# A state-space recurrence on one core: ScalarE instead of GpSimd copies each step's last states

## The chip, the cores and the metric

The kernel runs on one core of a Trainium2 chip. The metric is the device time of one execution in microseconds (us). Before the change the median of three runs is 3077.14 us (3073.25 to 3079.84).

The engines of a core are called PE (TensorE's matmuls; its weight loads are PEld), DVE (VectorE), ACT (ScalarE), POOL (GpSimd) and SP (SyncE, which here only issues DMAs). Each takes its instructions from a queue of its own and waits for the others through semaphores.

## What is computed

A block of two layers on 2 x 2048 tokens of width 256, all in float32: attention with 16 heads plus a mixture of 8 experts, then a state-space layer plus a ternary linear layer. Only the state-space layer is touched. Cut to what matters:

```python
x = silu(causal_conv(x) + conv_b)                 # 512 channels
dt = softplus(dt_low @ dt_proj_w.T + dt_proj_b)
def step(h, (dt_t, B_t, C_t, x_t)):               # h: 512 channels x 16 states
    h = exp(dt_t * A) * h + dt_t * B_t * x_t
    y = sum_over_states(h * C_t)
    return h, y
y = scan(step) + x * D
return (y * silu(z)) @ out_proj_w.T
```

The recurrence runs along time, from the first token of a sequence to its last.

## The kernel before

**Pieces.** A sequence is cut into 4 chunks of 512 tokens. A chunk of one of the two sequences is a piece here (the code calls it a unit and counts it by `at`), so there are 8 pieces, 0 to 7, the two sequences in turn. The last states of a chunk have to reach the next chunk of the same sequence, two pieces later. They are kept in `carry[b]`, a small tile per sequence.

**Steps.** A piece is worked off in 16 steps n = 0 to 15, 128 steps G = 0 to 127 in the whole kernel. A step holds 4 x 512 values on each of the 128 partitions (128x2048), four channel groups side by side. Step G is made of

- `decays` (L1729), four ACT activations 128x511 that write exp(dt A) into `decay[G % 2]`;
- `spread_b` (L1740), a PE matmul that spreads B over the partitions into the PSUM tile `bb`;
- `product` (L1753), a DVE multiplication that writes uh = dt x B into PSUM;
- L1841, a DVE addition on 128x4 elements, which puts the states carried in from the chunk before (`c0`) into uh;
- the scan (L1843), one DVE instruction over 128x2048, which writes the states hh (three buffers);
- the copy (L1854) of the last column of each group, 128x4 elements, from hh to `carry[b]`; and behind it on POOL
- the multiplication of hh in place by C (L1855, POOL, 128x2048);
- `summed` (L1770), PE matmuls that sum hh over the states into `y`, issued one step later.

Every fourth step ACT copies the finished `y` out of PSUM (`taken`, L1782).

**What fills the time between.** While the steps of a piece run, the pieces ahead are made ready and the one behind is finished. `mix` gathers expert outputs (L1302, indirect DMAs issued by POOL; L1311 scales them on ACT; L1316 adds them on POOL), adds the residual (L1379 POOL) and normalises (L1389, L1390 ACT; L1391 DVE; L1396, L1399 ACT). `ahead` projects (L1426 ACT takes the result), convolves by matmuls (L1446; L1455 ACT takes the result), applies Silu (L1461), computes the low-rank dt (L1466 PE, L1474 and L1475 ACT, L1535 PE, L1540 ACT), softplus (L1551 to L1563 on ACT, L1556 and L1561 on DVE) and dt and dt x (L1581, L1584 on POOL), spills both to DRAM (L1569) and reads them back spread over the partitions (`dd`, L1694). `first` makes `c0` for four steps from `dd` and `carry` (L1710 POOL, L1717 ACT, L1720 POOL). `behind` gates the finished piece (L1590 POOL, in two parts, which read the tile `xs` of that piece) and projects it out. In the first piece dt and dt x of its first channels are spread by matmuls instead (L1517, taken by ACT and DVE at L1520).

**The order is written by hand.** The scheduler is switched off for this part, so the order of the program text is the order of each engine's queue. Tables (`kinds0` for the first piece, `kinds` for the others) say at which step n and at which of four places q = 0 to 3 of that step a generator (`mix`, `ahead`, `behind`) advances by one stage. The loop of step G issues, in this order: `spread_b(G + 1)`, two `decays(G + 1)`, the stages of place 0, L1841 and the scan of G, two more `decays(G + 1)`, the stages of place 1, the copy L1854, the multiplication L1855, `summed(G - 1)`, the stages of place 2, `product(G + 1)`, the stages of place 3, `taken(G - 1)`. Results of matmuls are taken out of PSUM one stage late, from two buffers.

Of the kernel before, what the change touches and what calls it, by code (L numbers as in the profile page):

```python
# [25 lines left out]
CH = 512  # L26
# [75 lines left out]
def tile_model(ctx: ExitStack, tc: tile.TileContext, t, out):  # L102
# [55 lines left out]
    with ExitStack() as c0:  # L158
# [176 lines left out]
        experts(tc, t, col, row, ident, ones, xa, xa_d, rot, rw, x_d, y_d, routes)  # L335

    mix_and_state_space(
        tc, t, col, row, ident, ones, rot, routes, sab, rw, y_d, ab_d, xa_d, out_tiles
    )
# [808 lines left out]
def mix_and_state_space(tc, t, col, row, ident, ones, rot, routes, sab, rw, y_d, ab_d, xa_d, out_tiles):  # L1148
# [10 lines left out]
    nc = tc.nc  # L1159
# [7 lines left out]
    with ExitStack() as ctx:  # L1167
# [90 lines left out]
        carry, tail = [], []  # L1258
# [367 lines left out]
        def behind(at):  # L1626

            (c, b), m_ = units[at], of[at]
            if at > 0:
                gated(at - 1, slice(0, NB - 1))  # L1630
            yield
            if at > 0:
                gated(at - 1, slice(NB - 1, NB))
            yield
            out = leave(at - 1) if at > 0 else iter(())
            for _ in range(4):
                next(out, None)
                yield
            for _ in out:
                pass  # L1640
            zs = m_["zs"] = one.tile(full, F32, tag="zs", name=f"zs_{b}_{c}")
            for m in range(NB):
                issued(
                    project(NB + m, m_["xnT"], f"z_{b}_{c}_{m}"),
                    lambda ps, m=m: nc.scalar.copy(zs[:, m, :], ps),
                )
                yield
            settle()
            nc.scalar.activation(zs, zs, AF.Silu)
            yield  # L1650
# [39 lines left out]
        def spread(at, m):  # L1690

            dd = two.tile([P, 2, 4, CH], F32, tag="dd", name=f"dd_{at}_{m}")
            for r in range(4):
                nc.sync.dma_start(dd[C4 * r : C4 * (r + 1)], of[at]["dd_d"][m])  # L1694
            of[at]["dd", m] = dd

        def c_rows(at, g):

            cc = bcp.tile([P, 1, CH], F32, tag="cc", name=f"cc_{at}_{g}")
            for r in range(4):  # L1700
                nc.sync.dma_start(
                    cc[C4 * r : C4 * (r + 1), 0, :], of[at]["c_d"][4 * g + r].partition_broadcast(C4)
                )
            of[at]["cc", g] = cc

        def first(at, m):

            m_ = of[at]
            a0 = one.tile([P, 4, 4], F32, tag="a0", bufs=2, name=f"a0_{at}_{m}")
            nc.gpsimd.tensor_tensor(  # L1710
                a0,
                a_neg[:, :, 4 * m : 4 * m + 4].rearrange("p q g -> p g q"),
                m_["dd", m][:, 0, :, 0].unsqueeze(1).to_broadcast([P, 4, 4]),
                ALU.mult,
            )
            yield
            nc.scalar.activation(a0, a0, AF.Exp)  # L1717
            yield
            c0 = one.tile([P, 4, 4], F32, tag="c0", bufs=2, name=f"c0_{at}_{m}")
            nc.gpsimd.tensor_tensor(c0, a0, carry[units[at][1]][:, 4 * m : 4 * m + 4, :], ALU.mult)  # L1720
            m_["c0", m] = c0
            yield
# [3 lines left out]
        def decays(G, q):  # L1726
            if G < NG:
                at, n = divmod(G, NU)
                nc.scalar.activation(  # L1729
                    decay[G % 2][:, q, 1:],  # L1730
                    of[at]["dd", n // 4][:, 0, q, 1:],
                    AF.Exp,
                    scale=a_neg[:, q, n : n + 1],
                )

        def spread_b(G):
            if G < NG:
                at, n = divmod(G, NU)
                bb = of[at]["bb", n] = ps_u.tile([P, 1, CH], F32, tag="bb", name=f"bb_{at}_{n}")
                nc.tensor.matmul(  # L1740
                    bb[:, 0, :],
                    lhsT=selb[B0:XR, (n % 4) * P : (n % 4 + 1) * P],
                    rhs=of[at]["b"][B0:XR, :],
                    start=True,
                    stop=True,
                )

        def product(G):

            if G < NG:  # L1750
                at, n = divmod(G, NU)
                uh = of[at]["uh", n] = ps_u.tile(full, F32, tag="uh", name=f"uh_{at}_{n}")
                nc.vector.tensor_tensor(  # L1753
                    uh, of[at]["dd", n // 4][:, 1], of[at]["bb", n].to_broadcast(full), ALU.mult
                )

        def summed(G):

            if G < 0:
                return  # L1760
            at, n = divmod(G, NU)
            m, g = divmod(n, 4)
            hh = of[at]["hh", n]
            if g == 0:
                of[at]["y"] = ps_y.tile([P, CH], F32, tag="y", name=f"y_{at}_{m}")
                nc.tensor.matmul(
                    of[at]["y"], lhsT=dmat[:, m, :], rhs=of[at]["xs"][:, m, :], start=True, stop=False
                )
            for q in range(4):
                nc.tensor.matmul(  # L1770
                    of[at]["y"][C4 * q : C4 * (q + 1), :],
                    lhsT=sel,
                    rhs=hh[:, q, :],
                    start=False,
                    stop=(g == 3),
                    tile_position=(0, C4 * q),
                )

        def taken(G):
            if G >= 0 and G % 4 == 3:  # L1780
                at, n = divmod(G, NU)
                nc.scalar.copy(of[at]["xs"][:, n // 4, :], of[at]["y"])  # L1782
# [23 lines left out]
        def steps(at, n, q):  # L1806
            for kind in places.get((at == 0, n, q), ()):
                next(flows[kind], None)

        starts = nothing  # L1810
        for G in range(NG):
            at, n = divmod(G, NU)
            (c, b), m_ = units[at], of[at]
            m, g = divmod(n, 4)
            more = at + 1 < len(units)
            if n == 0:
                flows = [
                    aheads[at + 1] if more else nothing,
                    behind(at),
                    mixes[at + 2] if at + 2 < len(units) else nothing,  # L1820
                    mixes[at + 3] if at + 3 < len(units) else nothing,
                    aheads[at + 2] if at + 2 < len(units) else nothing,
                ]
                if at == 0:
                    flows += [mixes[2], aheads[0], mixes[1]]
            if g == 0 and m + 1 < NB and G:
                spread(at, m + 1)
            if more and n == 12:
                spread(at + 1, 0)
            if more and m == NB - 1:  # L1830
                c_rows(at + 1, g)
            if g == 2 and G > 2 or G == 3:
                starts = first(at, m + 1) if m + 1 < NB else first(at + 1, 0) if more else nothing
            spread_b(G + 1)
            for q in range(2):
                decays(G + 1, q)
            if g >= 2 and G != 2:
                next(starts, None)
            steps(at, n, 0)
            uh = m_["uh", n]  # L1840
            nc.vector.tensor_tensor(uh[:, :, 0], uh[:, :, 0], m_["c0", m][:, g, :], ALU.add)  # L1841
            hh = m_["hh", n] = wk.tile(full, F32, tag="hh", bufs=3, name=f"hh_{at}_{n}")
            nc.vector.tensor_tensor_scan(  # L1843
                hh.rearrange("p q c -> p (q c)"),
                decay[G % 2].rearrange("p q c -> p (q c)"),
                uh.rearrange("p q c -> p (q c)"),
                0.0,
                ALU.mult,
                ALU.add,
            )  # L1850
            for q in range(2, 4):
                decays(G + 1, q)
            steps(at, n, 1)
            nc.gpsimd.tensor_copy(carry[b][:, n, :], hh[:, :, CH - 1])  # L1854
            nc.gpsimd.tensor_tensor(hh, hh, m_["cc", g].to_broadcast(full), ALU.mult)  # L1855
            summed(G - 1)
            if g == 2 and G > 2 or G == 3:
                next(starts, None)
            steps(at, n, 2)
            product(G + 1)  # L1860
            steps(at, n, 3)
            if G == 3:
                next(starts, None)
            taken(G - 1)
            if n == NU - 1:
                for x in flows[:3]:
                    for _ in x:
                        pass
# [98 lines left out]
```

## Time and profile before

The profile is that of one execution.

| | |
|---|---|
| median of the runs | 3077.14 us |
| the profiled execution's own time | 3080.93 us |
| its span, first to last instruction | 3079.2 us |
| state-space part: first scan starts, last scan ends | 2014.2 us, 3052.5 us |
| DVE busy, whole span | 2043.7 us (66%) |
| ACT busy, whole span | 1592.4 us (52%) |
| POOL busy, whole span | 1187.6 us (39%) |
| the copies L1854, all 128 together | 45.6 us |
| mean granted TensorE clock | 0.897 of full speed |

How to read it. In a timeline, a line gives the start in us from the span's beginning, the duration, the engine, the line of the code, the operation, the tiles written and read, shapes and the number of instructions merged; a bracket at the end gives idle time of the engine before it and what ended that idle time. In the list of groups, "x128 | 579.9, 4531 | 10.3" says 128 instructions, 579.9 us busy, 4531 ns each, 10.3 us of idle time just before them. A wait for several semaphores is put down to the one that came last. "The waits of a line" lists how long its engine sat idle before its instructions, and until which instruction.

### The profile page before, as it was taken

How to read it: one execution, taken by the hardware profiler on the slowest of the kernel's cores; microseconds unless marked ns; L12 is line 12 of the kernel's file. 1: busy time of each engine (PE TensorE's matmuls, PEld its weight loads, DVE VectorE, ACT ScalarE, POOL GpSimd, SP SyncE). 2: the span in 40 equal slices, each digit the busy share in tenths (PEclk: the TensorE clock that was granted, in tenths of full speed). 3: DMA queues.
4: the chain of work that ended last, by engine and by line, in shares of the span. 5: the costliest groups of instructions: out<-in, count | busy, mean ns of one | idle time of the engine just before them, and what ended most of it. 6: DMA issues, size and time to landing. Idle time of an engine off the chain costs nothing. (4 is left out here: it accounts for less than half of the span.)

```text
span 3079.2 us, 39986 instructions
## 1 busy us (share of the span) xinstructions
PE 2634.9 (86%) x15021; PEld 1493.3 (48%) x15021; DVE 2043.7 (66%) x2558; ACT 1592.4 (52%) x2546; POOL 1187.6 (39%) x934
## 2 busy tenths in 40 slices
PE   6887888999999999799999999577778888788747
PEld 4543433445444444488888888333333343333303
DVE  6576766888788888324111011258999999999996
ACT  3424555666566666422222222456766676666643
POOL 4313223010111011111111111247887978878775
PEclk9978988999999999899999999677887888879758
DMA  8843214112232220434345553323544535445350
GB/s 290 214 133 80 57 51 86 29 29 42 50 48 29 29 29 1 151 134 144 133 150 194 183 193 109 77 54 85 120 111 104 131 78 133 110 102 117 82 116 14
DMA packets 120614, 309.58 MB, mean 101 GB/s; under 512 B 28464, under 2 KB 70832, under 8 KB 102880
## 3 DMA queue, kind: packets, MB, share of 16 engines
q1 hardware_dynamic: 100496, 206.57, 28.3%
q0 software_dynamic: 18576, 99.24, 9.6%
q8 instruction: 122, 2.00, 0.3%
q10 hardware_dynamic: 1344, 1.16, 0.1%
q14 instruction: 76, 0.62, 0.1%
HBM read 228.51 MB, written 78.38 MB: 100 GB/s over the span
## 5 line engine op out<-in xcount | busy, mean ns | idle before, releaser
L758 ACT ACTIVATE p<-s 128x1024 f32<-128x1024 f32 (+3 forms) x640 | 563.2, 900 | 382.4 <-PE s L750 361.5
L665 DVE TENSOR_REDUCE best<-m 128x2 f32<-128x1024 f32 (+3 forms) x640 | 669.6, 1062 | 111.6 <-PE m L652 101.0
L1855 POOL TENSOR_TENSOR hh<-hh,cc 128x2048 f32<-128x2048 f32 x128 | 579.9, 4531 | 10.3
L1843 DVE TENSOR_TENSOR_SCAN hh<-decay,uh 128x2048 f32<-128x2048 f32 x128 | 565.9, 4421 | 23.8 <-ACT decay L1729 10.1
L705 PE MATMUL pv<-p,v 128*17 128x256 f32 (+1 forms) x4608 | 383.8, 379 | 49.0 <-POOL p L763 46.1
L763 POOL TENSOR_SCALAR_AFFINE_SELECT p<-p 128x256 f32<-128x256 f32 x256 | 103.3, 408 | 785.6 <-ACT p L758 784.5
L1729 ACT ACTIVATE decay<-dd,a_neg 128x511 f32<-128x511 f32 x512 | 332.9, 712 | 53.4 <-DVE hh L1843 52.8
L1118 ACT ACTIVATE hT<-h,b1s 128x256 f32<-128x256 f32 x296 | 137.7, 473 | 384.3 <-PE h L1111 384.3
L1132 DVE TENSOR_TENSOR yt<-o,b 128x512 f32<-128x512 f32 x37 | 25.6, 692 | 436.9 <-PE o L1124 436.9
L1753 DVE TENSOR_TENSOR uh<-dd,bb 128x2048 f32<-128x2048 f32 x128 | 293.6, 2294 | 21.5 <-PE bb L1740 11.6
L750 PE MATMUL s<-q,k 64*128 64x512 f32 (+3 forms) x1280 | 288.2, 437 | 22.9 <-DVE best L665 17.6
L652 PE MATMUL m<-k,q 64*128 64x512 f32 (+3 forms) x1280 | 281.6, 426 | 17.6 <-DVE best L665 8.9
L1111 PE MATMUL h<-xT,w 128*128 128x256 f32 x1184 | 276.1, 387 | 19.7 <-ACT hT L1118 8.1
L1124 PE MATMUL o<-w,hT 128*128 128x256 f32 x1184 | 262.7, 380 | 0.0
L1074 POOL DMA_INDIRECT w<-in_w,wrow x74 | 71.1, 961 | 479.2 <-PE h L1111 255.5
L1111 PEld LDWEIGHTS h<-xT,w 128*128 128x128 f32 x1184 | 226.7, 193 | 54.8 <-ACT hT L1118 8.5
L750 PE MATMUL s<-tops,onesr 64*128 64x512 f32 (+3 forms) x1280 | 248.5, 371 | 0.0
L1124 PEld LDWEIGHTS o<-w,hT 128*128 128x128 f32 x1184 | 225.7, 191 | 30.9
L1770 PE MATMUL y<-hh,sel 128*32 128x512 f32 x1024 | 162.1, 710 | 78.8 <-POOL hh L1855 78.6
L705 PEld LDWEIGHTS pv<-p,v 128*17 128x17 f32 x4608 | 107.9, 97 | 232.4 <-issue 113.5
L750 PEld LDWEIGHTS s<-q,k 64*128 64x128 f32 x1280 | 127.0, 188 | 168.1 <-DVE best L665 56.6
L652 PEld LDWEIGHTS m<-k,q 64*128 64x128 f32 x1280 | 129.3, 192 | 131.7 <-ACT p L758 68.1
(341 smaller groups left out, 3477.2 us busy)
## 6 DMA issues: line engine op xcount, KB each, us to landing
dd<-dd_d SPq DMA_DIRECT2D x120, 512.0 KB, 7.1
q<-qk_d SPq DMA_DIRECT2D x128, 128.0 KB, 5.1
k<-qk_d SPq DMA_DIRECT2D x128, 128.0 KB, 7.5
x_d<-zero SPq DMA_DIRECT2D x6, 1664.0 KB
xg<-x_d SPq DMA_DIRECT2D x37, 256.0 KB, 6.6
y_d<-yt SPq DMA_DIRECT2D x37, 256.0 KB
qk_d<-qp SPq DMA_DIRECT2D x16, 512.0 KB, 7.3
qk_d<-kp SPq DMA_DIRECT2D x16, 512.0 KB, 4.0
```

The costliest lines, as they stand in the source:

```text
L652: nc.tensor.matmul(ps[:, h, 0:n], lhsT=qT[hs, qs], rhs=kT[hs, c * CH : c * CH + n], start=True, stop=True, tile_position=(HP * h, 0),)
L665: nc.vector.tensor_reduce(best[:, i, :, c], ps[:, :, 0:n], AX.X, ALU.max)
L705: nc.tensor.matmul(pv[r0 : r0 + HS + 1, lo - f * HC : HC], lhsT=v[:, b * TPB + kb, 2 * pr + h, :], rhs=pt[:, h, lo:hi], start=(kb == 0), s ...
L750: nc.tensor.matmul(ps[:, h, off:CH], lhsT=(kT[hs, kb * P : (kb + 1) * P], onesr[hs, :])[i], rhs=(qT[hs, j * CH + off : (j + 1) * CH], tp[h ...
L758: nc.scalar.activation(pt[:, :, off:CH], ps[:, :, off:CH], AF.Exp, scale=float(HS) ** -0.5)
L1111: nc.tensor.matmul(ph, lhsT=w1[:, k * DF + f * P : k * DF + (f + 1) * P], rhs=xT[:, k, :], start=(k == 0), stop=(k == 1),)
L1124: nc.tensor.matmul(po[:, h, :], lhsT=hT[:, f, h * P : (h + 1) * P], rhs=w2[:, f * D : (f + 1) * D], start=(f == 0), stop=(f == NF - 1),)
L1729: nc.scalar.activation(decay[G % 2][:, q, 1:], of[at]["dd", n // 4][:, 0, q, 1:], AF.Exp, scale=a_neg[:, q, n : n + 1],)
L1753: nc.vector.tensor_tensor(uh, of[at]["dd", n // 4][:, 1], of[at]["bb", n].to_broadcast(full), ALU.mult)
L1770: nc.tensor.matmul(of[at]["y"][C4 * q : C4 * (q + 1), :], lhsT=sel, rhs=hh[:, q, :], start=False, stop=(g == 3), tile_position=(0, C4 * q),)
L1843: nc.vector.tensor_tensor_scan(hh.rearrange("p q c -> p (q c)"), decay[G % 2].rearrange("p q c -> p (q c)"), uh.rearrange("p q c -> p (q c)"),
L1855: nc.gpsimd.tensor_tensor(hh, hh, m_["cc", g].to_broadcast(full), ALU.mult)
```

## The change

One instruction per step moves from POOL's queue to ACT's.

```diff
             for q in range(2, 4):
                 decays(G + 1, q)
             steps(at, n, 1)
-            nc.gpsimd.tensor_copy(carry[b][:, n, :], hh[:, :, CH - 1])
+            nc.scalar.copy(carry[b][:, n, :], hh[:, :, CH - 1])
             nc.gpsimd.tensor_tensor(hh, hh, m_["cc", g].to_broadcast(full), ALU.mult)
             summed(G - 1)
```

The place in the program stays. In ACT's queue the copy of step G stands behind the `decays(G + 1)` and the stages of places 0 and 1, and ahead of those of places 2 and 3. It waits for the scan of step G, which writes what it reads. The multiplication L1855 overwrites hh in place and therefore waits for the copy; on POOL that was given by the queue, now it is a semaphore between ACT and POOL. `first` reads `carry` on POOL (L1720), so there is now such a wait there too, in both directions. The orders of PE, DVE and SP are the same as before, and no table load is added on ACT.

## The prediction

> **What bounds the kernel now.** I read the page first, then the waits of the copy's line L1854, then windows over single pieces, then the timelines of ScalarE (ACT), GpSimd (POOL) and VectorE (DVE) across a border between pieces. Only the stretch after 2014 us of the 3079.2 us span is touched.
>
> From the page, with count, busy us, mean ns:
>
> ```profile
> L1855 POOL TENSOR_TENSOR hh<-hh,cc 128x2048 f32<-128x2048 f32 x128 | 579.9, 4531 | 10.3
> L1843 DVE TENSOR_TENSOR_SCAN hh<-decay,uh 128x2048 f32<-128x2048 f32 x128 | 565.9, 4421 | 23.8 <-ACT decay L1729 10.1
> ```
>
> One piece (16 steps) in the windows view: width, then busy us of PE, PEld, DVE, ACT, POOL.
>
> ```profile
> 2575.00:2703.00 128.00, 105.25 (x347) 45.48 (x345) 118.31 (x65) 86.80 (x135) 106.28 (x57) 0.85 0.46 110
> ```
>
> DVE is the bound: 118.3 of 128 us, and about 0.27 us of short gaps per step make it nearly full. ACT has 41 us of room, POOL 22. So an engine that only sheds work gains little; whoever makes DVE wait costs time. The copy itself, from the waits of its line (duration min/median/max in ns):
>
> ```profile
> L1854 POOL COPY carry<-hh x128: 177/188/2167, 2018.8 to 3052.6; 128x4 f32<-128x4 f32 x128
> ...
>   DVE hh L1843: 147.0, 64
> ```
>
> Half the copies find POOL already waiting for the scan; there removing a copy gains nothing unless its replacement ends earlier.
>
> **Part by part: what leaves POOL.** 128 copies. Most cost 0.19 us plus 0.08 before the multiply behind them: 0.27. Eleven took 1.6 to 2.17, ten of them 2.16 to 2.17, always while a VectorE scalar_tensor_tensor (L1556, L1561) ran: at step 8 of one piece the copy ran 2632.99 to 2635.15, that instruction 2632.84 to 2635.10. The Trainium skill (SBUF — State Buffer, section Who interferes with whom) explains it: a VectorE instruction with two SBUF inputs shuts out a GpSimd one that reads SBUF, and ScalarE waits for nobody. Taken for the copy alone it promises 10 x 1.97 = 20 us of POOL. But the same rule catches the multiply behind it, which reads two SBUF tiles and began only 0.08 us after the copy. I take 0.27 us there too.
>
> **What ACT gets.** 128 copies of 128x4. Nearest rows: L1717, 128x16, 0.22 us; L1396, 128x1, 0.28. I take 0.22: 28 us in all, hidden in ACT's idle 41 us per piece, except where ACT is late.
>
> **The new wait.** The multiply L1855 overwrites hh, so it must now wait for ACT's copy. If ACT is idle that changes nothing: before, the multiply began 0.33 us after the scan (0.06 + 0.19 + 0.08); after, about 0.06 + 0.22 + 0.06. But the copy stands on ACT behind all of decays(G+1) and the work of places 0 and 1 of its step. From the instruction order and the timeline I took, per step, the end of ACT's last instruction ahead of the copy minus the scan's end. It is positive in about half of the steps. At step 15 it is 4.1, 7.0, 5.7, 7.2, 5.6, 1.5, 2.8, 0 us over the eight pieces. Border of pieces 3 and 4:
>
> ```profile
> 2566.67 1.33 ACT L1729 ACTIVATE decay<-dd,a_neg 128x511 f32<-128x511 f32 x2
> 2567.91 1.69 ACT L1311 ACTIVATE ys<-ys,wts 128x256 f32<-128x256 f32 x4
> 2569.50 0.57 ACT L1426 COPY xr<-in 128x512 f32<-128x512 f32 x1
> 2569.97 2.56 ACT L1729 ACTIVATE decay<-dd,a_neg 128x511 f32<-128x511 f32 x4
> 2572.43 0.57 ACT L1426 COPY xr<-in 128x512 f32<-128x512 f32 x1
> 2578.37 0.59 ACT L1782 COPY xs<-y 128x512 f32<-128x512 f32 x1 [5.37 <-PE y L1770]
> 2578.85 2.56 ACT L1729 ACTIVATE decay<-dd,a_neg 128x511 f32<-128x511 f32 x4
> 2581.56 0.69 ACT L1455 ACTIVATE xs<-cv,cols 128x512 f32<-128x512 f32 x1
> ```
>
> ```profile
> 2564.91 4.52 POOL L1855 TENSOR_TENSOR hh<-hh,cc 128x2048 f32<-128x2048 f32 x1
> 2569.40 3.43 POOL L1590 TENSOR_TENSOR zs<-xs,zs 128x1536 f32<-128x1536 f32 x1
> ...
> 2573.45 4.51 POOL L1855 TENSOR_TENSOR hh<-hh,cc 128x2048 f32<-128x2048 f32 x1
> 2577.93 2.36 POOL L1316 TENSOR_TENSOR ys<-ys 128x1024 f32<-128x1024 f32 x1
> 2580.24 1.28 POOL L1590 TENSOR_TENSOR zs<-xs,zs 128x512 f32<-128x512 f32 x1
> ```
>
> See that L1455 starts when the second L1590 ends: it overwrites what that reads. The copy of step 15 lands behind the four L1311, at 2569.6, so its multiply starts at 2569.85 instead of 2564.91. All behind it on POOL is back to back: L1590 ends at 2577.8, the next multiply at 2582.6, L1316 at 2584.9, the second L1590 at 2586.2: 4.7 us late.
>
> Here a rule speaks against the change: the skill (Perfetto Trace Analysis, note under Tensor Engine Instruction) calls ACT, DVE and GPSIMD strict FIFO. The row agrees: the decays at 2578.85 needed only the scan that ended at 2572.46, yet stood behind L1782. Were the copy free to pass, it would go at 2562.45 and this border would cost nothing; by the rule it costs what follows.
>
> **Where the 4.7 us go** (steps 1 to 8, piece 4). L1455 ends at 2587.0, the copy behind it at 2587.2, decays and the second L1455 at 2590.6; the scan of step 3 (2589.48 before) waits: **+1.2**. TensorE's second-next convolution waits for the first L1455 to free its PSUM tile, so convolution, y and the transpose slip 4.1 us; with them Silu, its two table loads and the decays of step 5, which end at 2606.65; the scan (2603.80) now could start at 2605.0: +1.65, **2.9** so far. The gate, xp (5.4 us) and dt matmuls are 4.3 to 4.5 late; their products wait for bb behind them in TensorE's queue, and uh of step 8 and the pn evacuation, which already waited 0.53 and 1.36 us for TensorE, move fully: **+3.7** by step 8. In pieces 2 and 5 the scan of step 5 waited for ACT already (0.65 us), so no slack softens it: **+4.4**. In piece 1 the slip at L1590 is 3.3 and 2.6 reach step 8. In pieces 6 and 7 the slip is at most 2.8 and covered.
>
> **A second wait.** At step 10 ACT loads the Sqrt table and computes L1389/L1390 just before the scan ends (L1390 2653.96, scan's end 2654.06). The copy is put ahead and holds them until after the scan: 0.28 + 0.22 + 1.28 + 0.30 + 0.2, so DVE's reciprocal L1391, first behind that scan, waits 2.2 us. Pieces 1 to 4 take this from later stalls: there POOL is 5 to 9 us behind at steps 11 to 13, and DVE waits 4.0 us for it at steps 14 to 16 anyway (1.41 + 1.21 + 1.42 in piece 4). Piece 5 has no such stall: +2.2. Piece 0 has it at step 12: +0.8.
>
> **The gain.** In pieces 1 to 4 the next piece's start hangs on POOL: multiply, xc, multiply, L1581, multiply, L1584, whose spill and reload feed L1710. Two copies lie in it: -0.55 each.
>
> **The first piece.** ACT reaches the copy of step 1 at 2038.6, 4.8 after the scan; the multiply ends at 2043.4, not 2040.1, and L1575, for which TensorE stood idle 8.6 us, is 3.3 late. Step 2's copy is late by 3.6 more behind the L1520, so L1581, L1584, the spill and L1422 are 6.8 late, and c0 (L1720), for which DVE waits 12.5 us at 2077.55, comes 6.7 late: **+6.7**. Step 13's late multiply delays L1710 and the Silu behind it: +0.6. With L1391: 8.1.
>
> **Sum.** Piece 0: 8.1; 1: 2.6 - 0.55 = 2.05; 2: 4.4 - 0.55 = 3.85; 3 and 4: 3.15 each; 5: 4.4 + 2.2 = 6.6; 6 and 7: 0. Together 26.9 us. The profiled execution took 3080.93 (span 3079.2 and 1.7 around it): 3107.8. The median of the runs shown is 3.8 lower, so 3104.
>
> **Rivals.** *Faster.* Place: POOL's chain at steps 8 to 14. If the late multiply of step 15 is absorbed, pieces 1 to 4 gain three to four copies each, 0.8 to 1.1 us: 3 to 5 us, 3073. For it: the page's chain of waits lists POOL carry with 1%. It decides where step 15's multiply slips less than about 1.2 us, the slack ahead of step 5's scan; the trace says 5.0. And the first piece's 6.7 us has no slack anywhere. Chance 4%.
> *Absorbed.* From steps 2 to 7 POOL waits 2.2 to 2.4 us per scan, three hh buffers leave a multiply some room, and the convolutions may catch up. Then only the first piece and L1391 in piece 5 are left, less the gain: 8.1 + 2.2 - 2.2 = 8, 3085; with less of the first piece, within 0.2%. Chance 14%.
> *Cascade.* ACT lateness breeds more: copies of steps 4 to 7 come 1 to 4 us after the scan now and later after the slip, y on TensorE waits, and the slip reaches step 8 at 7 us instead of 4: 4 x 3.5 more, and 3 in piece 1: 17 more, 3121. If a late multiply of step 7 then also holds off L1556, some 10 more. Chance 17%.
> *As summed*: 65%.
>
> **How the numbers follow.** About 0.2% (6 us) is what a measurement of this kernel can tell from no change. Faster 0.04; same 0.08 (part of the absorbed case); slower 0.88. The range, 3084 to 3128, takes in absorbed and cascade and leaves out the faster case and the tails. The copy's price, 0.19 to 0.28, moves the sum by under 3 us.
>
> **What would show it.** Right: POOL's L1855 preceded by idle time ended by ACT L1854; at step 15 that multiply 5 us later after its scan; in piece 0 DVE's waits before L1385 and before L1841 of step 4 grow by 3.3 us each, to 9 and 16; about 2 us before L1391 in pieces 1 to 5; more DVE time waiting for decays; last two pieces unchanged. The multiply of step 8 still starts 2.1 us or more after the scan. Wrong: the multiply of step 15 starts within 2 us of its scan, or piece length from 2316 to 2703 (129 us each) does not grow.

## The result, and the profile after

The changed kernel takes 3094.47 us (median of four runs, 3092.49 to 3099.28); the kernel before, run beside it, 3075.19. The ratio is 1.0063, with a 95% interval of 1.0047 to 1.0079: 19.4 us longer, 14.5 to 24.3. The profiled execution took 3099.28 us, its span 3097.6.

Groups of the page, after. The columns are count, busy us, mean ns, then idle time before and what ended it.

```profile
L1855 POOL TENSOR_TENSOR hh<-hh,cc 128x2048 f32<-128x2048 f32 x128 | 597.7, 4671 | 233.6 <-ACT carry L1854 193.0
L1843 DVE TENSOR_TENSOR_SCAN hh<-decay,uh 128x2048 f32<-128x2048 f32 x128 | 565.9, 4421 | 34.0 <-ACT decay L1729 20.3
L1753 DVE TENSOR_TENSOR uh<-dd,bb 128x2048 f32<-128x2048 f32 x128 | 293.6, 2294 | 13.8 <-PE bb L1740 3.0
```

POOL now stands idle 233.6 us ahead of its multiplication, 193.0 of them until the copy on ACT ends. Part of that was there before, as waiting for the scan ahead of the copy (147.0 us). What counts is DVE, the bound: it works as long as before (2044.0 us in the whole span, before 2043.7), so the loss is what its idle time grew by. Ahead of the scan that is 10.2 us (23.8 to 34.0), and what ACT's decays end of it doubled. Ahead of the reciprocal L1391 it is 10.0 more, 14.7 instead of 4.7, but ahead of L1753 it is 7.7 less (before: 21.5): a good part of the reciprocal's wait is given back later.

The waits of the copy's line, after; the first kept line is what ACT waits for ahead of it, the second who waits for it:

```profile
L1854 ACT COPY carry<-hh x128: 178/196/204, 2025.2 to 3069.6; 128x4 f32<-128x4 f32 x128
...
  DVE hh L1843: 156.9, 55
...
  POOL hh L1855: 193.0, 55
```

In 55 of 128 steps ACT is early and waits for the scan. In 55 steps POOL waits for ACT. No copy takes 2 us any more.

One piece in the windows view, piece 4 as before (width, then PE, PEld, DVE, ACT, POOL):

```profile
2587.00:2718.00 131.00, 103.39 (x343) 45.32 (x342) 118.78 (x66) 88.04 (x152) 103.44 (x41) 0.86 0.45 109
```

DVE's work is the same 118 us (118.78, before 118.31), but the piece is 3 us wider. The border of pieces 3 and 4 on ACT and on POOL, after:

```profile
2577.94 1.69 ACT L1311 ACTIVATE ys<-ys,wts 128x256 f32<-128x256 f32 x4
2579.54 0.18 ACT L1854 COPY carry<-hh 128x4 f32<-128x4 f32 x1
2579.62 0.58 ACT L1426 COPY xr<-in 128x512 f32<-128x512 f32 x1
...
2595.92 0.69 ACT L1455 ACTIVATE xs<-cv,cols 128x512 f32<-128x512 f32 x1 [7.35 <-POOL zs L1590]
2596.50 0.19 ACT L1854 COPY carry<-hh 128x4 f32<-128x4 f32 x1
2596.59 1.33 ACT L1729 ACTIVATE decay<-dd,a_neg 128x511 f32<-128x511 f32 x2
```

```profile
2579.80 4.54 POOL L1855 TENSOR_TENSOR hh<-hh,cc 128x2048 f32<-128x2048 f32 x1 [5.32 <-ACT carry L1854]
2584.28 3.48 POOL L1590 TENSOR_TENSOR zs<-xs,zs 128x1536 f32<-128x1536 f32 x1
2587.67 0.22 POOL L1430 COPY tail<-xr 128x12 f32<-128x12 f32 x1
2587.82 4.54 POOL L1855 TENSOR_TENSOR hh<-hh,cc 128x2048 f32<-128x2048 f32 x1
2592.29 2.37 POOL L1316 TENSOR_TENSOR ys<-ys 128x1024 f32<-128x1024 f32 x1
2594.60 1.28 POOL L1590 TENSOR_TENSOR zs<-xs,zs 128x512 f32<-128x512 f32 x1
```

This is the predicted chain. The copy of step 15 runs behind the four L1311. Its multiplication starts 5.7 us after its scan (before: about 2.5), POOL is back to back up to the second L1590, and when that ends L1455 goes on ACT, for which ACT has stood idle 7.35 us. Counted from the end of step 0's scan, the two L1590 end 4.9 and 4.3 us later than before, and L1455 starts 4.3 later; the prediction had 4.7. Counted from its own scan the multiplication of step 15 is only 3.2 us later, not 5: the copy came 5.5 us after that scan, not 7.2, while step 0's scan now follows that of step 15 more closely (8.4 us after it instead of 10.0).

**Piece by piece.** Lengths from the end of step 0's scan to that of the next piece's step 0, in us. To keep the chance of one execution apart from the change, both kernels were traced twice more (runs before_b, before_c, after_b, after_c below), so each figure is a mean of three traces.

| piece | before | after | difference | predicted |
|---|---|---|---|---|
| 0 | 166.40 | 171.10 | 4.7 | 8.1 |
| 1 | 127.90 | 130.66 | 2.8 | 2.05 |
| 2 | 128.93 | 130.09 | 1.2 | 3.85 |
| 3 | 127.75 | 130.65 | 2.9 | 3.15 |
| 4 | 128.49 | 130.89 | 2.4 | 3.15 |
| 5 | 124.00 | 129.33 | 5.3 | 6.6 |
| 6 | 119.24 | 119.15 | -0.1 | 0 |
| 7 (to its last scan) | 107.32 | 107.34 | 0 | 0 |

Together 19.2 us; the timed runs show 19.4. By halves: in pieces 1 to 5 the first eight steps grow by 3.1, 2.0, 4.0, 3.0 and 3.1; the last eight shrink by 0.3, 0.8, 1.1 and 0.6 in pieces 1 to 4 and grow by 2.2 in piece 5.

### The profile page after: what moved, and what is told of

The parts are those of the page before. It is cut to its first block, busy times and chain, and to the rows that moved or that the text cites. A ratio compares the mean times of both kernels' runs of the same rounds, so it can differ in the third digit from the quotient of the medians.

```text
span 3097.6 us, 40026 instructions
## 1 busy us (share of the span) xinstructions
PE 2636.1 (85%) x15021; PEld 1495.6 (48%) x15021; DVE 2044.0 (66%) x2558; ACT 1604.6 (52%) x2674; POOL 1161.6 (38%) x806
## 5 line engine op out<-in xcount | busy, mean ns | idle before, releaser
L1855 POOL TENSOR_TENSOR hh<-hh,cc 128x2048 f32<-128x2048 f32 x128 | 597.7, 4671 | 233.6 <-ACT carry L1854 193.0
L1753 DVE TENSOR_TENSOR uh<-dd,bb 128x2048 f32<-128x2048 f32 x128 | 293.6, 2294 | 13.8 <-PE bb L1740 3.0
```

The source lines that it names most:

```text
L1753: nc.vector.tensor_tensor(uh, of[at]["dd", n // 4][:, 1], of[at]["bb", n].to_broadcast(full), ALU.mult)
```

## The experiments

Three theories stood. **A**, the prediction's: the multiplication L1855 has to wait for copies that come late, above all that of step 15, and a copy put ahead of L1389 holds up the reciprocal. **B**: ACT's 28 us of added work are the price, wherever they lie. **C**: what stands behind the copy in ACT's queue is held while the copy waits for its scan. Us in this section are the ratio times the 3076 us of the kernel before, with the 95% interval.

**Step 15 alone (only15), and all but step 15 (not15).**

```diff
-            nc.gpsimd.tensor_copy(carry[b][:, n, :], hh[:, :, CH - 1])
+            if n == 15:            # not15: if n != 15
+                nc.scalar.copy(carry[b][:, n, :], hh[:, :, CH - 1])
+            else:
+                nc.gpsimd.tensor_copy(carry[b][:, n, :], hh[:, :, CH - 1])
```

> Only the copies of step 15 (8 of 128) go to ScalarE, the others stay on GpSimd. Theory A (a late copy holds up GpSimd's multiplication, and the late multiplication of step 15 holds up the convolutions of the next piece): the slip of steps 1 to 8 in pieces 1 to 5 stays, 13 to 14 us in the trace after the change, so about 3089, with the rises at steps 3 to 8 and none at step 11. Rival B (the copies' own time on ScalarE, 128 x 0.19 = 25 us): 8 copies, 1.5 us, 3077. Rival C (ScalarE's own later work is held behind the wait for the scan): nothing is held at step 15, where the copy itself comes late: 3075.

> All copies but those of step 15 go to ScalarE. Theory A: the first piece (4.3 us in the trace after the change) and the reciprocal at step 10 in piece 5 (2.2) stay, less 0.5 to 1 us of GpSimd's gain in each of pieces 1 to 4: about 3079, and pieces 1 to 4 no longer than before. Rival B: 120 of 128 copies, 23 us, 3097. Rival C: unchanged from all copies on ScalarE, about 3094.

Measured: only15 3090.48 us, ratio 1.0048 (1.0034 to 1.0062), +14.8 us (10.5 to 19.1). not15 3082.49 us, ratio 1.0015 (1.0005 to 1.0024), +4.6 (1.5 to 7.4). Eight copies make 14.8 us and the other 120 make 4.6, which together is the 19.4 of the whole change. The waits of only15's eight ACT copies:

```profile
L1855 ACT COPY carry<-hh x8: 181/183/197, 2179.4 to 3061.2; 128x4 f32<-128x4 f32 x8
...
  POOL hh L1858: 31.4, 8
```

Eight copies of 0.18 us make POOL wait 31.4 us. B is out: a sixteenth of the load brings three quarters of the loss. In not15 pieces 2, 3 and 4 are shorter than before (126.64, 126.97 and 126.54 us). Not all of that is POOL's gain: 0.7, 0.9 and 0.4 us of it lie in the last eight steps, where the prediction has that gain, and in pieces 2 and 4 another 1.6 in the first eight, in piece 2 from step 5 on, where TensorE ran faster (see the part on steps 1 to 8 below). Its piece 0, with no copy of step 15 on ACT, took 174.30 us, longer than in any of the three traces of the changed kernel.

**All but step 10 (not10)**, as above with `n != 10`.

> All copies but those of step 10 go to ScalarE. Theory A: the wait of 2.1 us before the reciprocal goes in pieces 1 to 5, but only piece 5 keeps the gain, since pieces 1 to 4 lose it to later stalls on GpSimd: 2.2 us less than with all copies on ScalarE, about 3092. Rival C: 2.1 us in each of five pieces, 10 less, about 3084. Rival B: 1.5 less, 3093.

Measured: 3096.71 us, ratio 1.0068 (1.0054 to 1.0082), +20.9 (16.6 to 25.2); a miss for A's number. In the trace the jump at step 11 is gone as A said (piece 5 is 127.05 us, not 129.3). But the last eight steps of pieces 1 to 4 shrink less: 68.3, 67.9, 68.4 and 67.8 us, where the changed kernel has 67.9, 67.5, 67.7 and 67.4. Together that is 1.9 us, against the 2.2 gained in piece 5. Step 10's copy is back in POOL's queue there; that this is what takes it back is argued, not tested. Nothing is left that can be measured.

**Wait and load apart (apart).** All copies are on ACT, as in the change. GpSimd multiplies 511 of the 512 columns; ACT scales the last column in place, behind its own copy. So the multiplication waits for nobody on ACT, while ACT has 128 instructions more than in the change.

```diff
-            nc.gpsimd.tensor_copy(carry[b][:, n, :], hh[:, :, CH - 1])
-            nc.gpsimd.tensor_tensor(hh, hh, m_["cc", g].to_broadcast(full), ALU.mult)
+            nc.scalar.copy(carry[b][:, n, :], hh[:, :, CH - 1])
+            nc.scalar.activation(hh[:, :, CH - 1], hh[:, :, CH - 1], AF.Copy, scale=m_["cc", g][:, 0, CH - 1 : CH])
+            ct = m_["cc", g][:, :, 0 : CH - 1].to_broadcast([P, NB, CH - 1])
+            nc.gpsimd.tensor_tensor(hh[:, :, 0 : CH - 1], hh[:, :, 0 : CH - 1], ct, ALU.mult)
```

> All copies go to ScalarE, but GpSimd's multiplication leaves out the last column (511 of 512 columns), and a second small ScalarE activation, behind the copy, multiplies that column by its C in place: so GpSimd no longer waits for ScalarE, while ScalarE waits and works as before and does one instruction more per step. The output is the same. Theory A: the slip at steps 1 to 8 and the first piece's loss go, the 2.2 us at the reciprocal in piece 5 and 0.8 in piece 0 stay, GpSimd's gain of 0.5 to 1 us per piece stays: 3072 to 3078. Rival B: twice the instructions, 25 to 50 us more than before: 3100 to 3125. Rival C: as with all copies on ScalarE, 3094.

Measured: 3074.16 us, ratio 0.9996 (0.9988 to 1.0004). The whole 19 us are gone. The multiplication's line in apart, with what its idle time waits for:

```profile
L1857 POOL TENSOR_TENSOR hh<-hh,cc x128: 4492/4532/6436, 2020.8 to 3054.8; 128x2044 f32<-128x2044 f32 x128
...
  DVE hh L1843: 148.9, 60
```

It waits for the scan, not for ACT. A stands; B and C fall as the main cause. C's part remains in small: from step 10 to 11 the scans still slip by 2.5 us, which is the reciprocal's wait; most of it is given back later in pieces 1 to 4, and in the time nothing is left over.

**ACT's load alone (load).** The kernel before, with 128 ACT copies of 128x4 from a constant tile, waiting for nothing (`idle` is a small tile set to 0 beforehand, which the cut leaves out).

```diff
+            nc.scalar.copy(idle[:, 1, :], idle[:, 0, :])
             nc.gpsimd.tensor_copy(carry[b][:, n, :], hh[:, :, CH - 1])
```

> The kernel before, whose copies stay on GpSimd, with 128 further ScalarE copies of 128x4 from a constant tile at the same place in the order: they wait for nothing and nobody waits for them. A (ScalarE's time doesn't matter, only what waits for the copy): 0.09 to 0.2 us each where ScalarE's decays are just in time, so 0 to 2 us, 3075 to 3077. B (ScalarE's load is the price): 3090 to 3095, as in the changed kernel.

Measured: 3076.88 us, ratio 1.0003 (0.9994 to 1.0011), at most 3.4 us by the interval. As A has it; B is out.

**The wait without the relief (both).** The kernel before, and beside each copy an ACT copy of the same elements to a tile that nobody reads. POOL's multiplication waits for it, and POOL sheds nothing.

```diff
             nc.gpsimd.tensor_copy(carry[b][:, n, :], hh[:, :, CH - 1])
+            nc.scalar.copy(idle[:, 1, :], hh[:, :, CH - 1])
```

> The kernel before, whose copies stay on GpSimd, and beside each a ScalarE copy of the same 128x4 out of hh into a tile that nobody reads: GpSimd's multiply waits for it as in the changed kernel, but GpSimd sheds nothing. A (the wait of the multiply makes the loss, and shedding a copy from GpSimd gives 0.5 to 1 us in each of pieces 1 to 4): the changed kernel's 3094.5 plus 2 to 4: 3096 to 3099. D (shedding the copies gains nothing): 3094 to 3095. B (shedding costs, for instance because carry is written by another engine): under 3090.

Measured: 3104.71 us, ratio 1.0097 (1.0082 to 1.0112), +29.8 (25.2 to 34.5): 10 us above the change, where A expected 2 to 4. The sign is A's, the size is not. In the trace the last eight steps of pieces 1 to 4 take 68.3, 68.4, 69.0 and 68.1 us, 3.3 more than in the changed kernel: the expected part. Another 4.5 lie in piece 0, 175.6 us to 171.1, but there one trace is a weak witness: ahead of L1556 in step 1 DVE waits 6.38 us, as in the first trace of before and in not15, and 4.57 in the three of the changed kernel. That is 1.8 of the 4.5. So shedding the copies is worth something in the first piece too (about 2 us, worked out below), and the timed runs say that it is worth more than I thought; where all 10 us come from is not settled.

**All but the first piece (notfirst)**, as only15 with `at > 0`.

> The 16 copies of the first piece stay on GpSimd, the other 112 go to ScalarE. A (each loss sits where one late copy lands, and the sums of the pieces are separate): the first piece's +4.8 us goes, pieces 1 to 5 lengthen as in the changed kernel (1.3, 1.4, 2.8, 2.5, 4.6), so about 3075 + 12.6 = 3088 to 3090, and DVE's waits before L1385 and before L1841 of step 4 stay at 5.8 and 12.5 us. B (ScalarE is simply loaded with 28 us): 112 of 128 copies, so 7/8 of 19.3 us: 3092. C (the loss grows with each late copy by way of the next piece): a punctual first piece also saves part of the later ones, under 3085.

Measured: 3086.57 us, ratio 1.0038 (1.0024 to 1.0052), +11.7 (7.4 to 16.0). The first piece's copies make some 8 of the 19 us. My expectation of 3088 to 3090 put the piece borders wrongly: step 15 of piece 0 belongs to these copies and its loss falls into piece 1. In the trace both happen: piece 0 is 165.85 us as before, and piece 1, which the change lengthens by 2.8, takes 126.86.

**Both ACT instructions later in the step (later).** As apart, with the two ACT instructions behind place 2 of the step.

```diff
             steps(at, n, 2)
+            nc.scalar.copy(carry[b][:, n, :], hh[:, :, CH - 1])
+            nc.scalar.activation(hh[:, :, CH - 1], hh[:, :, CH - 1], AF.Copy, scale=m_["cc", g][:, 0, CH - 1 : CH])
```

> All copies on ScalarE, GpSimd multiplies the first 511 columns of hh only, and a second ScalarE instruction scales the last column in place; both stand behind the third place of each step in ScalarE's order, not behind its second. Output as before. A (the multiply no longer waits for ScalarE, and behind place 3 the two instructions no longer stand between the Sqrt load and L1389/L1390): no jump of 2.1 us at step 11, the gain of 0.5 to 1 us in pieces 1 to 4 kept: 3070 to 3073, below both kernels. C (ScalarE's own order of place costs nothing or moves the stall elsewhere: sums of step n+3 or the buffer of hh wait for the last column): 3076 to 3085.

Measured: 3075.11 us, ratio 0.9995 (0.9987 to 1.0003). The jump at step 11 is gone, as A said (from step 10 to 11 the scans shift by -0.1 us against before, not +2.1), but the time misses A's 3070 to 3073: it is better than the change and cannot be told from the kernel before. Nor from apart: with the reciprocal's wait or without it, the time is the same, as not10 has it too. The gain in the last eight steps is under 0.4 us in pieces 1 to 3 and none in piece 4, not 0.5 to 1 each; why it is smaller than in the changed kernel, no run here shows.

**Each kernel traced twice more (before_b, before_c, after_b, after_c)**, unedited.

> The kernel before, unedited, for a second trace of it. A (the half-speed stretches of TensorE fall differently in each execution, so part of the shortfall of the predicted sum is the one trace it was read from): its scans stand 1.5 us or more earlier than in the first trace by the end of the first piece, and pieces 1 to 5 differ from the first trace by up to 2.6 us each, as in the kernel with 128 idle copies. E (the stretches belong to the kernel): every piece within 0.3 us of the first trace.

> The kernel before once more. As for the one ahead of it: A: first piece 0 to 1.6 us shorter than in the first trace, pieces 1 to 5 scattered by up to 2.6 us. E: within 0.3 us.

> The changed kernel, unedited, for a second trace of it. A: the first piece lengthens by 3 to 8 us against the first trace of before (four traces with its copies moved gave 4.8, 6.9, 3.4, 8.2), pieces 1 to 5 by 11 to 15 together, pieces 6 and 7 by nothing; the stretch from step 5 to step 8, which the prediction had at +0.8, scatters between -1 and +1.3. E: every piece within 0.3 us of its first trace.

> The changed kernel once more. As for the one ahead of it: A: first piece 3 to 8 us longer than in the first trace of before, pieces 1 to 5 together 11 to 15. E: within 0.3 us of its first trace.

Measured, one execution each: 3078.20, 3071.52, 3092.54, 3097.17 us. Neither theory holds for every piece. Pieces 2, 3, 4, 6 and 7 of before agree within 0.2 us over the three traces, so there E is right. Pieces 0, 1 and 5 of the first trace are 1.5, 2.8 and 1.5 us longer than the mean of the other two: the trace that I predicted from was a slow draw in three places. The changed kernel's pieces 1 to 5 make 11.0 and 11.4 us more than in the first trace of before, at the lower edge of what A gave.

## Why the prediction was right or wrong, point by point

**The cause was right.** The time is lost because POOL's multiplication waits for a copy that stands behind other work on ACT (apart takes that wait away and adds to ACT's work, and the loss goes), most of it at step 15 (only15), none of it through ACT's load (load). The rivals fall: Faster, because step 15's multiplication slips by 3 to 5 us; Cascade, because no slip bred more than 4.0 us by step 8 on the mean of three traces. Absorbed is true in part: pieces 2 and 5 pass on less than was said, as the next points show.

**The sum was 26.9 us and the traces give 19.2.** Of the 7.7 too many, 3.4 are in the first piece, 3.6 in steps 1 to 8 of the later pieces, 0.7 in the gain. The terms that were mis-sized:

*The first piece, 8.1 by the prediction, 4.7 by the traces.* DVE's waits in the first piece, before and then after:

```profile
2045.00 0.43 DVE L1385 BATCH_NORM_STATS2 st<-xc 128x6 f32<-128x256 f32 x1 [5.78 <-POOL xc L1379]
...
2077.55 0.17 DVE L1841 TENSOR_TENSOR uh<-uh,c 128x4 f32<-128x4 f32 x1 [12.53 <-POOL c L1720]
```

```profile
2046.05 0.43 DVE L1385 BATCH_NORM_STATS2 st<-xc 128x6 f32<-128x256 f32 x1 [8.90 <-POOL xc L1379]
...
2063.99 2.30 DVE L1753 TENSOR_TENSOR uh<-dd,bb 128x2048 f32<-128x2048 f32 x1 [1.54 <-PE bb L1740]
2081.82 0.17 DVE L1841 TENSOR_TENSOR uh<-uh,c 128x4 f32<-128x4 f32 x1 [15.54 <-POOL c L1720]
```

The two signs came nearly as written, 8.9 and 15.5 where 9 and 16 were said. That they were right and the sum was not has three reasons. First, the gain on POOL's side was counted in pieces 1 to 4 alone. With the wait and no relief (both) the first piece takes 8.2 us more than in the first trace of before, which has the same long wait in step 1: 3.2 at step 2, 3.4 at step 4, 1.4 at its end. The prediction said 6.7 for the first two and 0.6 for the last. With the relief (after_b against before_b) these are 3.1, 2.7 and 0.7, and step 13's wait before L1385 falls from 1.80 to 1.06 us: three times 0.7 back, about 2 us. Second, step 12's reciprocal, put at +0.8, waits 0.60 us in both kernels: nothing. Third, at step 7 before_b waits 6.72 us for ACT's L1475 and after_b 5.52: the eight matmuls L1466 ahead of it took 6.42 us in the one and 5.22 in the other, and that draw of TensorE's speed alone makes 1.2 us.

*Steps 1 to 8 of pieces 1 to 5, 18.8 by the prediction, 15.2 by the traces.* Pieces 1, 3 and 4 gave 10.1 where 10.0 was said; that it fits so well is luck, for one by one they gave 3.1, 4.0 and 3.0 where 2.6, 3.7 and 3.7 were said. Pieces 2 and 5 gave 2.0 and 3.1 where 4.4 was said for each. The step that failed is "no slack softens it" in pieces 2 and 5. There the scan of step 5 waited 0.65 us for ACT already, and I took that wait for a property of the kernel. In piece 5 it was a draw of the one execution: the third trace has no such wait, nor the second. The scan of step 5 of piece 5 in the first trace of before, then in the second:

```profile
2733.22 4.42 DVE L1843 TENSOR_TENSOR_SCAN hh<-decay,uh 128x2048 f32<-128x2048 f32 x1 [0.65 <-ACT decay L1729]
```

```profile
2728.66 4.42 DVE L1843 TENSOR_TENSOR_SCAN hh<-decay,uh 128x2048 f32<-128x2048 f32 x1
```

In piece 2 the wait is there in all three traces, but behind it stands TensorE at half speed. The last of the four convolutions (L1446) in piece 2, before and then after:

```profile
2332.94 5.40 PE L1446 MATMUL cv<-xr,taps 128*128 128x512 f32 x8
```

```profile
2342.81 3.70 PE L1446 MATMUL cv<-xr,taps 128*128 128x512 f32 x8
```

It starts 4.1 us late, counted from step 0's scan, and ends 2.4 us late, because the same eight matmuls ran 1.70 us faster. The two stretches in the windows view (the third column from the end is the granted clock), before and after:

```profile
2332.90:2338.40 5.50, 5.50 (x13) 2.14 (x16) 5.41 (x2) 0.34 (x2) 3.23 (x4) 0.69 0.99 223
```

```profile
2342.80:2346.60 3.80, 3.80 (x13) 1.59 (x16) 3.50 (x4) 1.30 (x4) 3.80 (x3) 1.00 1.02 220
```

In piece 2 this is no chance: 5.40 us in all three traces of before, 3.70 in all three of after. In piece 5 only the first trace of before had 5.40, the other five have 3.70. But the half speed did not go away, it moved: in the changed kernel it is the convolution ahead that ran slowly, 5.72 us instead of 3.70 in the first trace (5.35 and 3.70 in the others):

```profile
2335.70:2341.40 5.70, 5.66 (x10) 2.24 (x10) 5.14 (x4) 3.92 (x9) 5.50 (x3) 0.64 0.91 269
```

So a slip on TensorE need not be passed on whole: where the slow stretch falls decides how late the last convolution ends. A late start is not needed for full speed: in not15, apart and later the last convolution of piece 2 starts 17.2 us after step 0's scan, as before, and takes 3.70. What decides where the stretch falls, no run here settles. The rest of the shortfall is the +0.8 between steps 5 and 8, of which piece 2 shows nothing and piece 5 0.7.

*Step 3, 1.2 by the prediction, 0.3 measured.* Three small terms were too large: L1455 is 4.3 us late, not 4.7; in the ACT lines above the copy starts at 2596.50 and the decays behind it at 2596.59, so it takes 0.09 us of the queue, not 0.2; and the four decays and L1455 behind it take 3.1 us, not the 3.4 in the sum. This cost nothing in the end, since step 5 decides.

*The reciprocal L1391: right.* Step 10 of piece 4, ACT, then DVE, after:

```profile
2667.38 0.20 ACT L1854 COPY carry<-hh 128x4 f32<-128x4 f32 x1 [3.27 <-DVE hh L1843]
2667.48 0.21 ACT L1717 ACTIVATE a<-a 128x16 f32<-128x16 f32 x1
2667.71 1.28 ACT L1389 ACT_TABLE_LOAD   x1
2669.00 0.30 ACT L1389 ACTIVATE r<-mv,eps 128x4 f32<-128x4 f32 x1
2669.33 0.20 ACT L1390 ACTIVATE r<-r 128x4 f32<-128x4 f32 x1
```

```profile
2669.57 0.20 DVE L1391 RECIPROCAL r<-r 128x8 f32<-128x8 f32 x1 [2.23 <-ACT r L1390]
```

The copy waits 3.27 us for the scan, and the table load and L1389 stand behind it; before, the reciprocal waited 0.14 us. Kept in piece 5 (+2.2), given back in pieces 1 to 4, as said.

*The gain, 0.55 in each of pieces 1 to 4: somewhat small.* The traces give 0.3, 0.8, 1.1 and 0.6 for the last eight steps, together 2.9 before rounding, where 2.2 was said, net of the L1391 stall.

**One sign was read wrongly.** The multiplication of step 8 does not start 2.1 us after its scan. It starts at once and lasts longer; POOL, then DVE, after:

```profile
2646.78 6.02 POOL L1855 TENSOR_TENSOR hh<-hh,cc 128x2048 f32<-128x2048 f32 x1 [0.25 <-ACT carry L1854]
```

```profile
2646.12 2.27 DVE L1556 SCALAR_TENSOR_TENSOR dt<-dt,s 128x2048 f32<-128x2048 f32 x1
```

DVE's two-input L1556 ended at 2648.39; the multiplication ends 4.4 us after that, which is about its usual length (4.53). The argument behind the sign held: the rule of the Trainium skill (SBUF — State Buffer, section Who interferes with whom), taken for the copy alone, promised POOL 20 us, and the multiplication behind it pays instead. L1855's busy time grew by 17.8 us (579.9 to 597.7). The block has moved from the copy's duration into the multiplication's.

**The starting point.** The prediction was built on an execution of 3080.93 us whose pieces 0, 1 and 5 were a slow draw. Setting off from the median, 3.8 us lower, took most of that out of the total, but not out of the terms. Of the 9.5 us between 3104 and 3094.5, 7.5 are the sum's and 2 are the kernel before, whose median beside the changed one was 3075.2, not 3077.1.

## What to carry to other kernels

An instruction moved to another in-order queue takes that queue's lateness with it: what counts is not its duration but when the new engine reaches it, and who must not overwrite its input until then. Here eight instructions of 0.18 us cost 15 us; one column taken out of the waiting instruction's range made the wait go away, though ACT then had more to do. And before a wait is carried through a chain, ask of each link whether its duration is fixed, and look at more than one trace; here TensorE's was not, and a wait read from one trace was missing in the next.

## What the runs showed of the hardware

Matmuls of one form take 592 or up to 1221 ns within one piece (L1446 in piece 2 of the changed kernel; the granted clock is 1.00 over one convolution and 0.64 over the other). The same eight, unedited, take 3.70 or 5.40 us in different executions (piece 5 of the kernel before), and whole pieces spread by 1.5 us (piece 0) and 2.9 (piece 1). The Trainium skill (TensorE: Matmul & The Clock Gate, section What's actually happening) says why executions may differ: a free-running window of about 3.4 us decides the clock. That agrees with piece 5 and says nothing on why piece 2 was the same three times; that the clock makes the whole spread of pieces 0 and 1 is not shown.

A 128x4 ACT copy between other ACT instructions shows 0.19 us in the trace and delays what follows by 0.09.

POOL's instructions that read SBUF while DVE's two-input L1556 ran were lengthened: the 128x4 copy took 2.16 us instead of 0.19 before, the 128x2048 multiplication 6.02 instead of 4.53 after.
